# Cross-attention and FFN on one core: the first later group's keys as seven whole block products

## The chip, the cores and the metric

The kernel runs on one NeuronCore of a Trainium2 chip. The core has five engines with instruction queues of their own: TensorE (PE; its weight loads are listed apart as PEld), VectorE (DVE), ScalarE (ACT), GpSimd (POOL) and SyncE (SP, which here only starts transfers). They meet through semaphores. The metric is the device time of one execution in microseconds (us); the median of several executions is compared.

## The reference

The input `x` has 8 sequences of 128 rows by 512. One layer of cross-attention with a context of the same shape, then a gated feed-forward layer, each behind a layer norm, in fp32:

```python
x = x + _L0_xattn_ref(_layernorm(x), ctx_4096, mask, position_bias, ln_weight, w_q, w_k, w_v, w_out)
x = x + _L0_ffn_ref(_layernorm(x), Wg, Wu, Wd, ag, au, ad)
...
h_k = (key_value_states @ w_k.T).reshape(b, lk, H, DH)
h_v = (key_value_states @ w_v.T).reshape(b, lk, H, DH)
score = jnp.einsum('bqhd,bkhd->bhqk', h_q, h_k) + position_bias[None]
score = jax.nn.softmax(jnp.where(m, score, -jnp.inf), axis=-1)
attn = jnp.einsum('bhqk,bkhd->bqhd', score, h_v).reshape(b, lq, H * DH)
out = attn @ w_out.T
```

There are 32 heads of 128, so keys, values and queries are each a product of 1024 by 512 with 512 by 4096. The change touches only how the keys of heads 4 to 7 are computed, not what they are.

## The kernel before

**Groups and stages.** The 32 heads are worked in 8 groups of 4. First come the keys and values of group 0, then the queries of all groups (stored to memory and fetched back in pairs of sequences), then attention, group by group and within a group sequence by sequence (a "batch", b = 0 to 7), then output projection and feed-forward. While group g is in attention, the keys and values of group g+1 are projected in pieces between the batches: in group 0 these are `k1` and `v1`.

**Block products.** A projection is done as a 2 by 2 block product with seven products in place of eight (Winograd's form of Strassen's scheme). The sums of weight blocks, `S`, are made on GpSimd by `combine_rows` (L312); those of the context's blocks were made once. `seven` (L334) runs all seven, in the order 2, 1, 6, 7, 4, 5, 3, each in two tiles of 128 by 512: 14 tiles. A tile goes to a PSUM bank and is read out from there: products 2, 6, 7 and 4 are copied by ACT, products 1, 5 and 3 are added to what is there by VectorE. Product 2 has a pair of banks of its own, products 1, 6, 7 and 4 are accumulated one after the other in a second pair, 5 and 3 in a third. So a tile must wait until the tile before it in its bank has been read out, and only two banks are held at a time.

**Parted products.** `four` (L364) runs only products 1, 6, 7 and 5 as whole tiles: 8 tiles. Products 2, 3 and 4 are parted once more, each into seven small ones, run together by `inner` (L384) in seven steps of three 128x256 products, with two additions on VectorE each. The small products need further sums: of the weights' blocks (`inner_rows` in `later_kv`, L601, eight sums on GpSimd, written to `s_k` or `s_v`) and of the context's blocks (`inner_tokens`, L433, four sums `t_c` on VectorE for each of products 2, 3 and 4, used again by all later groups).

**The order.** `later_kv` (L594) is a generator. Each `next` issues a tile or a step and gives its cost (`FULL` 4 for a tile, `PART` 3 for a step). It also issues what the next pieces need: `begin(n + 1)` makes the `S` of the next projection, and `inner_rows` and `inner_tokens` come at set tiles. For `k1` (n = 0): `begin` of `v1` ahead of tile 4, the context sums of product 4 ahead of tile 5 (those of 2 and 3 ahead of tile 1), `inner_rows` ahead of tile 6. The steps begin behind tile 7 and alternate with tiles; the steps left over run between the tiles of the next projection.

The attention loop (from L889) calls it. In group 0, two tiles are issued ahead of batch 0. In each of batches 0 to 3, `probabilities` (L496) issues the scores `sc` on TensorE, the masked addition `s`, the row maximum `mx` and its negative `nmx` on VectorE, then one piece (`ahead`), the four exponentials on ACT, one piece (`between`), and then `ri`, its reciprocal and `p` on VectorE. `transpose_p` turns `p` in blocks on VectorE (`tt`) and by two transfers through memory (`turned`, `pT`). `advance(3)` multiplies with the values (`av`) three batches later. Further pieces follow until their costs reach `due(g, b)` (L870). For group 0 this is 5, 8, 11 and 14 tiles' cost behind batches 0 to 3; from batch 4 on it runs evenly to the end of the group.

The masks (`s` from `pb` and `mneg`, 128 by 512, on GpSimd) are made two batches ahead into three buffers, so the mask of batch b + 3 waits for `p` of batch b. In batches 0 to 3 of group 0 every engine's instructions are kept in the order of the code (class `InOrder`, L54); most of these rows bear its line, L62.

Of the kernel before, what the change touches and what calls it, by code (L numbers as in the profile page):

```python
# [36 lines left out]
class Later:  # L37
# [10 lines left out]
    def next(self, engine):  # L48
        if self.calls:
            op, args, kw = self.calls.pop(0)  # L50
            getattr(engine, op)(*args, **kw)
# [15 lines left out]
def xattn_ffn_kernel(  # L67
# [26 lines left out]
    NG = H // GH  # L94
# [201 lines left out]
    def sums_a(eng, a11, a12, a21, a22, s1, s2, s4):  # L296

        eng.tensor_tensor(s1, a21, a22, ADD)
        eng.tensor_tensor(s2, s1, a11, SUB)
        eng.tensor_tensor(a21, a11, a21, SUB)  # L300
        eng.tensor_tensor(s4, a12, s2, SUB)
        return {1: a11, 2: a12, 3: s4, 4: a22, 5: s1, 6: s2, 7: a21}
# [9 lines left out]
    def combine_rows(name, w):  # L312

        a11, a12 = w[:, :HC, :HW], w[:, HC:, :HW]
        a21, a22 = w[:, :HC, HW:], w[:, HC:, HW:]
        s = spool.tile([P, 3, HC, HW], F32, tag="S", name=f"S_{name}")
        s1, s2, s4 = s[:, 0], s[:, 1], s[:, 2]
        rows = sums_a(gpsimd, a11, a12, a21, a22, s1, s2, s4)
        rows["lower"] = w[:, HC:]
        return rows  # L320
# [43 lines left out]
    def four(name, product, part, pool=ps_mm, tag="mm"):  # L364

        m = None
        for i, to in ((1, [(1, 1)]), (6, [(1, 2)]), (7, [(2, 2), (2, 1)]), (5, [(2, 2), (1, 2)])):
            if i in (1, 5):
                m = [pool.tile([P, 512], F32, tag=tag, name=f"mm_{name}_{i}_{t}") for t in range(2)]
            for t in range(2):  # L370
                product(i, t, m[t], i in (1, 5))
                for r, c in to:
                    if i == 5:
                        vector.tensor_tensor(part(r, c, t), part(r, c, t), m[t], ADD)
                    else:
                        scalar.copy(part(r, c, t), m[t])  # L376
                yield
# [55 lines left out]
    def inner_tokens(eng, src, half, place, products=SINGLE):  # L433

        blocks = {}
        for n in products:
            b = [src[n][:, c, at] for c in range(2) for at in (slice(0, half), slice(half, None))]
            b11, b12, b21, b22 = b
            t1, t2, t3, t4 = place(n)
            eng.tensor_tensor(t1, b12, b11, SUB)  # L440
            eng.tensor_tensor(t2, b22, t1, SUB)
            eng.tensor_tensor(t3, b22, b12, SUB)
            eng.tensor_tensor(t4, b21, t2, SUB)
            blocks[n] = numbered(*b, t1, t2, t3, t4)
        return blocks
# [143 lines left out]
            yield next(values)  # L589
        yield from values  # L590

    FULL, PART = 4, 3

    def later_kv():  # L594


        def place(n):
            t = ipool.tile([P, 4, HW], F32, tag=f"t{n}", name=f"t_c{n}")
            return (t[:, k] for k in range(4))

        def inner_rows(name, w):  # L601

            s = ipool.tile([P, 3, 3, P], F32, tag="rows", name=f"s_{name}", bufs=2)
            lower = w["lower"].rearrange("p c (n r q) -> p c n r q", n=2, r=2)
            both = [lower[:, c, :, r] for r in range(2) for c in range(2)]
            three = [w[3][:, c, bass.ts(r, P)] for r in range(2) for c in range(2)]
            sums = sums_a(gpsimd, *both, *(s[:, k, :2] for k in range(3)))
            a = {n: {i: rows[:, k] for i, rows in sums.items()} for k, n in enumerate((2, 4))}
            a[3] = sums_a(gpsimd, *three, *(s[:, k, 2] for k in range(3)))
            return a  # L610

        todo = [(g, kind) for g in range(1, NG) for kind in "kv"]
        made, rows = {}, {}

        def begin(n):

            g, kind = todo[n]
            if g not in made:
                made[g] = dict(zip("kv", kv_w.pop(g)))
            rows[n] = combine_rows(f"{kind}{g}", made[g].pop(kind))  # L620

        begin(0)
        b, steps = inner_tokens(vector, ctx_t, HW, place, (2, 3)), iter(())
        for n, (g, kind) in enumerate(todo):
            name, w = f"{kind}{g}", rows.pop(n)
            out = kvs.setdefault(g, ([], []))["kv".index(kind)]
            if g + 1 < NG:
                blocks, smaller = (blocks_T, inner_T) if kind == "k" else (blocks_V, inner_V)
                tiles = four(name, *blocks(name, w, ctx_t, out))
            else:  # L630
                tiles = (project_T if kind == "k" else project_V)(name, w, ctx_t, out)
            for k in itertools.count():

                if k == (3 if n == 0 else 5) and n + 1 < len(todo):
                    begin(n + 1)
                if n == 0 and k == 4:
                    b.update(inner_tokens(vector, ctx_t, HW, place, (4,)))
                if k == (5 if n == 0 else 2) and g + 1 < NG:
                    a = inner_rows(name, w)
                if next(tiles, "none") == "none":  # L640
                    break
                yield FULL
                if k == 6 and g + 1 < NG:
                    steps = smaller(name, a, b, out)
                if next(steps, None):
                    yield PART
# [36 lines left out]
    for n, _ in enumerate(first_kv()):  # L683
        if n in moments_at:
            pair[moments_at[n]] = norm1_moments(moments_at[n])
        if n in scales_at:
            b = scales_at[n]
# [6 lines left out]
        if n in turns_at:  # L694
            b = turns_at[n]
# [174 lines left out]
    def due(g, b):  # L870


        tiles, steps = 2 * 8 * FULL, 2 * 7 * PART
        late = 5 * PART
        if g == 0 and b < 4:
            return (5 + 3 * b) * FULL
        if g < NG - 2:
            start = 14 * FULL if g == 0 else g * (tiles + steps) - late
            end, n, k = (g + 1) * (tiles + steps) - late, 4 if g == 0 else B, b - 4 if g == 0 else b
        else:  # L880
            start, n, k = g * (tiles + steps) - late, B, b
            end = start + late + 25 * FULL
        return start + (end - start) * (k + 1) / n - 1.5

    todo = [(g, i) for g in range(NG) for i in range(B // 2)]
# [3 lines left out]
    for g in range(NG):  # L889
# [6 lines left out]
        if g == 0:  # L896
            products = later_kv()
# [11 lines left out]
        for b in range(B):  # L909
# [49 lines left out]
            if g == NG - 1:  # L959
                while next(products, None):  # L960
                    pass
            else:
                while done < due(g, b):
                    done += next(products)
# [11 lines left out]
            if g == NG - 1:  # L976
# [9 lines left out]
                n = (b + 2) % B, (b + 2) // B  # L986
# [481 lines left out]
```

## Time and profile before

| what | value |
|---|---|
| median of 3 runs | 1083.56 us (1082.39 to 1084.94) |
| the profiled execution | 1083.05 us, of which the span from first to last instruction is 1081.1 us |
| mean granted TensorE clock | 0.998 |
| TensorE in 239.17 to 295.20 us (group 0 in attention) | busy 53.03 of 56.03 us, clock 0.97 |
| TensorE in 295.20 to 355.50 us (group 1) | busy 59.70 of 60.30 us |
| TensorE in 355.50 to 415.70 us (group 2) | busy 60.20 of 60.20 us |

Busy times say how long an engine had an instruction in work. TensorE's rows overlap at their ends, so a group's work is best taken from start to start. A row of the timeline has the start in us, the time in us, the engine, the line, the operation with its result and its sources, and in brackets how long the engine stood idle before it and what released it. A row of the waits has who waited for whom, then the total, the count and the longest.

### The profile page before, as it was taken

Reading aid. Unit: us, or ns where it says so; the run is one execution under the profiler, and the core shown is the slowest. Engines: PE = TensorE matmul, PEld = TensorE weight load, DVE = VectorE, ACT = ScalarE, POOL = GpSimd, SP = SyncE. Lnnn points to the kernel's source line nnn. Section 1 sums busy time; section 2 is a strip of 40 time slices with the busy share of each in tenths; the row PEclk is TensorE's granted clock in tenths of the full one; section 3 lists DMA queues with packets and bytes.
Section 4 is the critical chain, followed back from the end, with each engine's and each line's share of the span. In section 5 each row is a group of like instructions: output and inputs, shape, how many; then the busy total and the mean of one; then the engine's idle time right before and its main releaser. Section 6 shows DMA issues by size and latency. Waiting matters only on the chain.

```text
span 1081.1 us, 14017 instructions
## 1 busy us (share of the span) xinstructions
PE 1070.5 (99%) x4874; PEld 806.3 (75%) x4874; DVE 696.2 (64%) x1280; ACT 331.4 (31%) x902; POOL 463.7 (43%) x519
## 2 busy tenths in 40 slices
PE   9999999998999999999999999999999999999998
PEld 5656666656978788887979768988888865665787
DVE  4653443437888888788877876984444338778732
ACT  2633323213544444444444334221000012332100
POOL 6233454533564545555551363662000326784010
PEclk9999999999999999999999999999999999999999
DMA  9613344453755555465555556873541622110011
GB/s 289 194 58 117 116 159 168 179 190 132 234 203 186 168 171 177 160 205 166 186 186 197 192 177 213 278 242 124 189 142 60 192 103 59 40 49 10 1 39 39
DMA packets 124693, 161.82 MB, mean 150 GB/s; under 512 B 15600, under 2 KB 77296, under 8 KB 124624
## 3 DMA queue, kind: packets, MB, share of 16 engines
q1 hardware_dynamic: 110208, 129.73, 36.4%
q10 hardware_dynamic: 12544, 24.38, 6.3%
q0 software_dynamic: 1872, 6.82, 2.1%
q8 instruction: 39, 0.64, 0.2%
q14 instruction: 30, 0.25, 0.1%
HBM read 104.81 MB, written 56.10 MB: 149 GB/s over the span
## 4 chain that ended last, share of the span: by engine, by line
PE 88%; DVE 6%; DMA 3%; ACT 1%; issue 1%; POOL 0%; SPq 0%; ACTq 0%; DVEq 0%; POOLq 0%
PE mm_q L454 10%; PE m L835 9%; PE mm_v L475 8%; PE mm_k L454 8%; PE m L62 7%; PE d L1389 6%; PE mm_f L1288 6%; PE i_q L403 6%; PE i_v L416 5%; PE i_k L403 4%; PE av L552 4%; PE sc L504 4%; PE i L1254 3%; PE mm_v L62 2%; PE mm_k L62 1%
## 5 line engine op out<-in xcount | busy, mean ns | idle before, releaser
L516 ACT ACTIVATE s<-s,nmx 128x128 f32<-128x128 f32 x240 | 93.3, 390 | 59.4 <-DVE nmx L511 46.8
L493 POOL TENSOR_TENSOR s<-pb,mneg 128x512 f32<-128x512 f32 x40 | 50.9, 1274 | 128.0 <-DVE p L527 104.6
L398 DVE TENSOR_TENSOR q<-q,i_q 128x512 f32<-128x512 f32 x98 | 49.9, 550 | 82.1 <-PE i_q L403 81.7
L557 ACT COPY aT<-av 128x512 f32<-128x512 f32 x60 | 35.1, 586 | 149.9 <-PE av L552 118.1
L527 DVE TENSOR_TENSOR p<-s,ri 128x512 f32<-128x512 f32 x52 | 63.6, 1223 | 1.4
L376 ACT COPY q<-mm_q 128x512 f32<-128x512 f32 x56 | 31.5, 588 | 94.6 <-PE mm_q L454 67.4
L504 PEld LDWEIGHTS sc<-k,q 128*128 128x128 f32 x416 | 54.1, 192 | 8.1 <-issue 6.5
L62 POOL TENSOR_TENSOR s<-pb,mneg 128x512 f32<-128x512 f32 x24 | 30.4, 1272 | 67.3 <-DVE p L527 41.0
L454 PE MATMUL mm_q<-hT,wq 128*128 128x512 f32 x128 | 58.5, 592 | 0.0
L475 PE MATMUL mm_v<-wv,ctx_sb 128*128 128x256 f32 x240 | 56.2, 380 | 0.6 <-ACT v L345 0.6
L454 PE MATMUL mm_q<-hT,S_q 128*128 128x512 f32 x120 | 55.9, 592 | 0.0
L552 PE MATMUL av<-pT,v 128*128 128x128 f32 x416 | 55.1, 275 | 0.6 <-DMA pT<-turned 0.6
L504 PE MATMUL sc<-k,q 128*128 128x128 f32 x416 | 55.3, 275 | 0.0
L62 POOL TENSOR_TENSOR S_q<-wq 128x512 f32<-128x512 f32 x8 | 10.1, 1268 | 104.4 <-ACT wq L62 104.4
L475 PE MATMUL mm_v<-S_v,ctx_sb 128*128 128x256 f32 x232 | 54.6, 380 | 0.0
L398 DVE TENSOR_TENSOR v<-v,i_v 128x512 f32<-128x512 f32 x84 | 43.8, 540 | 13.9 <-PE i_v L416 13.3
L454 PE MATMUL mm_k<-ctx_sb,wk 128*128 128x512 f32 x112 | 52.5, 593 | 0.0
L552 PEld LDWEIGHTS av<-pT,v 128*128 128x128 f32 x416 | 50.6, 192 | 0.8 <-ACT s L516 0.8
L62 PE MATMUL m<-wo,a 128*128 128x256 f32 x200 | 48.8, 380 | 0.9 <-DMA a<-att 0.9
L475 PEld LDWEIGHTS mm_v<-wv,ctx_sb 128*128 128x128 f32 x240 | 44.8, 190 | 6.4 <-ACT v L345 0.8
L454 PE MATMUL mm_k<-ctx_sb,S_k 128*128 128x512 f32 x104 | 48.6, 593 | 0.0
L835 PE MATMUL m<-wo,a 128*128 128x256 f32 x200 | 48.4, 379 | 0.0
(376 smaller groups left out, 2547.1 us busy)
## 6 DMA issues: line engine op xcount, KB each, us to landing
queries<-q SPq DMA_DIRECT2D x32, 512.0 KB, 3.8
turned<-tt SPq DMA_DIRECT2D x64, 256.0 KB, 2.8
pT<-turned SPq DMA_DIRECT2D x64, 256.0 KB, 3.2
att<-aT ACTq DMA_DIRECT2D x64, 256.0 KB, 3.0
q<-queries SPq DMA_DIRECT2D x30, 512.0 KB, 5.1
a<-att SPq DMA_DIRECT2D x23, 512.0 KB, 4.4
wq<-in_wqT_dram SPq DMA_DIRECT2D x8, 1024.0 KB, 6.8
wk<-in_wkT_dram SPq DMA_DIRECT2D x7, 1024.0 KB, 5.4
```

Source lines behind the costliest of these rows:

```text
L62: return self.tc.keep_in_program_order(getattr(self.engine, op)(*args, **kw))
L398: vector.tensor_tensor(to, to, out, ADD)
L403: kv_tensor.matmul(out, a[n][i], b[n][i], start=first, stop=True, skip_group_check=True)
L454: kv_tensor.matmul(out, w[i][:, c, bass.ts(t, P)], src[i][:, c, :], start=(first and c == 0), stop=(c == HC - 1), skip_group_check=True,)
L475: kv_tensor.matmul(out[:, bass.ts(k, HW)], src[i][:, c, bass.ts(2 * t + k, S)], w[i][:, c, :], start=(first and k == 0 and c == 0), stop=( ...
L504: tensor.matmul(sc[:, j, :], qT[:, j, bass.ts(b % 2, S)], kT[j][:, cols], start=True, stop=True)
L516: scalar.activation(s[:, j, :], s[:, j, :], AF.Exp, bias=nmx[:, j : j + 1], accum_out=sm[:, j : j + 1],)
L527: vector.tensor_tensor(p.rearrange("q h (j r) -> q h j r", r=BS), s.rearrange("q h (r j) -> q h j r", r=BS), ri.unsqueeze(2).unsqueeze(3). ...
L552: tensor.matmul(av[:, j, :], v[b // 2][:, b % 2, bass.ts(j, P)], pT[:, :, j, :], start=True, stop=True,)
L835: tensor.matmul(m[n], sa[n][:, c, :], wo_t[g][n][:, c, :], start=(g == order[0] and c == 0 and PRODUCTS.index(n) % 2 == 0), stop=(g == ord ...
L1288: nc.tensor.matmul(out, ws[t][n][:, c, :], h2_t[n][:, :, c, :], start=(first and c == 0), stop=(c == HC - 1), skip_group_check=True,)
L1389: nc.tensor.matmul(out, lhs, rhs, start=bank not in started, stop=(i == NP - 1 or n == 8), skip_group_check=True,)
```

## The change

`k1`, the first projection that `later_kv` makes (n = 0), now runs through `seven` in 14 whole tiles rather than through `four` and seven steps of small products. All others stay parted (but those of the last group, which were whole before). `begin` of `v1` stands ahead of tile 6 rather than tile 4. The context sums of product 4 stand ahead of tile 11 rather than tile 5. `inner_rows` isn't called for `k1`. A tile of `k1` is counted at 3.8 (`FIRST`), and the due costs of the first four batches are counted in it too.

```diff
--- before.py
+++ after.py
@@ -589,7 +589,9 @@
             yield next(values)
         yield from values
 
-    FULL, PART = 4, 3
+
+
+    FULL, PART, FIRST = 4, 3, 3.8
 
     def later_kv():
 
@@ -624,23 +626,24 @@
         for n, (g, kind) in enumerate(todo):
             name, w = f"{kind}{g}", rows.pop(n)
             out = kvs.setdefault(g, ([], []))["kv".index(kind)]
-            if g + 1 < NG:
+            parted = 0 < n and g + 1 < NG
+            if parted:
                 blocks, smaller = (blocks_T, inner_T) if kind == "k" else (blocks_V, inner_V)
                 tiles = four(name, *blocks(name, w, ctx_t, out))
             else:
                 tiles = (project_T if kind == "k" else project_V)(name, w, ctx_t, out)
             for k in itertools.count():
 
-                if k == (3 if n == 0 else 5) and n + 1 < len(todo):
+                if k == 5 and n + 1 < len(todo):
                     begin(n + 1)
-                if n == 0 and k == 4:
+                if n == 0 and k == 10:
                     b.update(inner_tokens(vector, ctx_t, HW, place, (4,)))
-                if k == (5 if n == 0 else 2) and g + 1 < NG:
+                if k == 2 and parted:
                     a = inner_rows(name, w)
                 if next(tiles, "none") == "none":
                     break
-                yield FULL
-                if k == 6 and g + 1 < NG:
+                yield FULL if n else FIRST
+                if k == 6 and parted:
                     steps = smaller(name, a, b, out)
                 if next(steps, None):
                     yield PART
@@ -873,7 +876,7 @@
         tiles, steps = 2 * 8 * FULL, 2 * 7 * PART
         late = 5 * PART
         if g == 0 and b < 4:
-            return (5 + 3 * b) * FULL
+            return (5 + 3 * b) * FIRST
         if g < NG - 2:
             start = 14 * FULL if g == 0 else g * (tiles + steps) - late
             end, n, k = (g + 1) * (tiles + steps) - late, 4 if g == 0 else B, b - 4 if g == 0 else b
```

## The prediction

> **What bounds the kernel now.** I read the page's busy shares first, then TensorE's own list of waits, then the timeline around those waits.
>
> ```profile
> PE 1070.5 (99%) x4874; PEld 806.3 (75%) x4874; DVE 696.2 (64%) x1280; ACT 331.4 (31%) x902; POOL 463.7 (43%) x519
> ...
> PE i_k L62 <- DVE k L62: 2.0, 1, 2.0
> PE i_k L403 <- POOL s L62: 1.0, 1, 1.0
> PE av L552 <- DMA pT<-turned: 0.6, 1, 0.6
> ```
>
> TensorE is busy 99% of the span, so work added to it costs its own length, and a stall removed is gained in full. Of the few stalls, the three shown lie in the stretch that the change rewrites: at 264.48, 260.93 and 296.87 us. The table of stretches (length, then busy times, then granted clock, DMA share, GB/s) shows a second loss:
>
> ```profile
> 257.90:265.00 7.10, 4.10 (x18) 3.01 (x17) 6.61 (x13) 1.11 (x6) 1.27 (x1) 1.00 0.24 76
> 265.00:270.00 5.00, 5.00 (x21) 4.45 (x20) 4.25 (x8) 1.05 (x5) 2.68 (x4) 0.66 0.14 52
> ```
>
> In half-microsecond stretches the clock is 0.50 from 265.5 to 268.9. From start to start the loss is: 1.14 us (259.79 to 260.93), 2.26 us (262.22 to 264.48), and at half clock 5.67 us for 3.90 us of work, 1.77. Together **5.2 us**, and 0.6 at 296.87. From 239.01 to the first scores of the next group at 295.0 there are 56.0 us; 50.8 of them are work.
>
> Why it stalls: the small products' additions stand in VectorE's strict order behind one batch's softmax and the four context sums `t_c`, and VectorE is busy 6.61 of 7.10 us.
>
> ```profile
> 250.48 1.27 POOL L62 TENSOR_TENSOR s<-pb,mneg 128x512 f32<-128x512 f32 x1 [11.28 <-DVE p L62]
> 251.00 1.03 DVE L62 TENSOR_TENSOR t_c<-ctx_sb 128x256 f32<-128x256 f32 x1
> 251.71 0.91 POOL L62 TENSOR_TENSOR s_k<-wk 128x256 f32<-128x256 f32 x1
> 252.06 0.83 DVE L62 TENSOR_TENSOR t_c<-ctx_sb,t_c 128x256 f32<-128x256 f32 x1
> ...
> 254.55 0.68 DVE L62 TENSOR_TENSOR s<-sc,s 128x512 f32<-128x512 f32 x1
> ...
> 278.54 1.28 POOL L62 TENSOR_TENSOR wk<-wk 128x512 f32<-128x512 f32 x1
> ...
> 278.97 0.87 DVE L523 TENSOR_SCALAR ri<-sm 128x4 f32<-128x4 f32 x1 [0.80 <-ACT s L516]
> ...
> 279.76 1.28 POOL L62 TENSOR_TENSOR S_k<-wk,S_k 128x512 f32<-128x512 f32 x1
> ...
> 280.08 1.83 DVE L527 TENSOR_TENSOR p<-s,ri 128x512 f32<-128x512 f32 x1
> ```
>
> Each of these VectorE rows ends after the GpSimd row that was running when it began. Beside an idle GpSimd `t_c` took 0.42 (239.71), `ri` 0.17 and `p` 1.09 (249.24). Four `t_c` took 3.55 us here; at the 0.35 spacing seen at 239.71 they would take 1.5.
>
> **TensorE's work.** A whole tile is 4 rows in 1.72 us, a small step 6 rows in 1.29. Before: 8 tiles and 7 steps, 13.76 + 9.03 = 22.8. After: 14 tiles, 24.1. **Plus 1.3 us**, and nothing hides it. Here a rule pulls the other way: the Trainium skill, "TensorE: Matmul & The Clock Gate", section "Back-to-back issue gap", gives sustained spacings of 131 ns at 512 columns and 81 at 128 (98 at 256, my linear estimate), so long matmuls are cheaper per column. By it the 24 long rows that replace 42 short ones would take 0.77 of their time, 6.9 us for 9.0, a gain of 2.1. In the rows here 512 columns take 0.43 us and 256 take 0.215: no discount. I take the row.
>
> **What is removed elsewhere.** 14 additions on VectorE and 8 small sums on GpSimd leave; VectorE's whole-tile additions rise from 4 to 6, ACT keeps 8 copies. These engines are not the bound on average; what counts is the order in which their pieces stand. No DMA is issued by the moved sums. The key weights are last read by tile 10 (about 259) and not by a step at 276.7, so the load behind them (SP at 277.39) can start earlier; its first reader is at 328, so that is worth nothing.
>
> **What is moved.** (a) The keys' smaller row sums go, and the value rows' four sums `S_v` (234.12 to 239.2 before, 1.27 each) move behind tile 5. On GpSimd they now follow the fourth mask, which waits for the first `p`. (b) The last four `t_c` move from behind the first batch to behind the third, ahead of tile 11's addition. (c) The order of products is now 2, 1, 6, 7, 4, 5, 3: product 3 is accumulated in product 5's bank, so **tile 13 waits for tile 11's addition** on VectorE.
>
> Now the order, in the durations of the rows. TensorE: tiles 1 and 2 until 242.44, scores 0 until 243.33, tiles 3, 4, 5 until 248.5, scores 1 (0.885) and tiles 6 to 8 until 254.5, scores 2 and tiles 9 to 11 until 260.6, scores 3 and tile 12 until 263.2. The copies on ACT come in time for all of these (the table load at 245.85 starts as soon as ACT is free, so it moves ahead of the first exponentials).
>
> VectorE: tile 4's addition ends at 247.7, `ri`, reciprocal, `p` (1.09) and transpose end at 250.0, against 251.08 before. Batch 1 takes 5.6 us (254.55 to 260.2 before) when nothing collides. But the fourth mask now runs 249.4 to 250.7 and `S_v` 250.7 to 255.85: `nmx` waits about 0.4, `ri` 0.6 and `p` 0.9, less what the pieces hide: end at 257.5 and not at 255.9, **1.6 us of collision**. Batch 2: 5.6, until 263.1. Its mask runs from 262.5, and right behind it on GpSimd follow the values' smaller row sums, which wait for nothing (they did so at 268.47, behind the mask of 267.24). So `t_c` stands beside the same pair as at 250.48: 3.55 us rather than 2.0 beside the mask alone, **1.5 us of collision**, until 266.65; tile 11's addition ends at 267.3. Tile 13 was ready at 263.2: **stall 4.1 us**. Bounds: 1.0 with neither collision, 4.6 if `p` waits a whole GpSimd row. I take 4.1, since both collisions are in the rows.
>
> The clock: the gap of 2.0 us brought 3.4 us at 0.50, the one of 0.98 nothing. The same page, section "Why this matters for your kernels", puts the limit at gaps of about 3 us; by that the old gap cost no clock, and the row contradicts it. The new gap is beyond both: 3.4 us at half clock, **1.7 us** (1.2 to 3.4, by where the gap meets the clock's own stretches).
>
> Behind it: tile 14 and scores 4 follow with VectorE ahead of them. Value tile 3 waits for ACT's copy of tile 1, which stands behind the exponentials of batch 4; `nmx` of that batch meets GpSimd's next sums at about 275. With half clock behind TensorE this is covered: 0.2 (0 to 1.7 if the clock stays whole). The wait at 296.87 goes: batch 5's `p` is about 2 us earlier relative to its use; kept, it costs 0.6.
>
> **The sum.** +1.3 work, +4.1 stall, +1.7 clock, +0.2 copy, -5.2 old stalls and clock, -0.6: **+1.5 us**. The groups behind show no idle TensorE between 300 and 580, so it is carried to the end. On the profiled execution's 1083.05 this gives **1084.6**. The median of the runs shown is 0.5 above that execution, inside their spread; I don't add it.
>
> **Rivals.**
> 1. *The collisions fail to happen* (the row sums stand elsewhere on GpSimd than I read). The stall is 1.0, the clock stays whole, the copy costs 0.6: 1.3 + 1.0 + 0.6 - 5.8 = -2.9, 1080.1. For it: 8 of VectorE's additions in net leave exactly this stretch. Against: the order on GpSimd is kept as written, and the rows show the waiting.
> 2. *Only the first collision.* Stall 2.6, clock whole as the page has it, copy 0.4: -1.5, 1081.5. By the row of 265.5 the clock halves and it is about 1083.2. The value sums' start at 268.47 speaks against.
> 3. *Slower: the gap at tile 13 spans a boundary of the clock's stretches*, so the clock is still judged idle once more and stays at half for 6.8 us: 1.3 + 4.1 + 3.4 + 0.2 - 5.8 = +3.2, 1086.3. It decides from 5.2 us at half clock on (cost 2.6). For it: a gap longer than 3.4 us must leave idle time in two stretches. Against: after the old gap one stretch was enough.
> 4. *That the change doesn't take the stalls away at all* is excluded in the place (the small steps of the keys are gone), not in the amount: that is the forecast.
>
> **Chances.** The forecast has 0.42, its own range 1083.2 to 1086.1; rival 3 has 0.22, rival 1 0.20, rival 2 0.16. A difference under 0.2% (2.2 us) of the median can't be told from none with this kernel. Faster: rival 1 and a quarter of rival 2, 0.24. Within: 0.24 of the forecast and the rest of rival 2, 0.36. Slower: 0.18 of the forecast and rival 3, 0.40. The range, 1080.3 to 1087.0, leaves out about half of rival 1 and a third of rival 3.
>
> **What would show it.** No small key products in the first group, 24.1 us of whole key tiles; one wait of 3.5 to 4.5 us at tile 13, its releaser an addition on VectorE; `t_c` at 0.8 to 1.0 each beside GpSimd; `p` of batch 1 at about 1.9; the clock at 0.50 for some 3.4 us behind 267; no wait of `av` at the head of the next group; that group's first scores at 296 to 297. If the wait at tile 13 is under 2 us, or the clock stays at 1.00, the forecast is wrong and the kernel is faster.

## The result, and the profile after

| | before | after |
|---|---|---|
| median (22 executions each) | 1083.32 us (1082.02 to 1085.54) | 1086.12 us (1084.01 to 1091.25) |
| the profiled execution, its span | 1083.05, 1081.1 us | 1087.1, 1085.3 us |
| tile 1 of the second group's keys starts at | 239.01 us | 239.19 us |
| the third group's second key tile (group 1's piece) starts at | 300.89 us | 305.54 us |

The ratio of the times is 1.0026 (1.0019 to 1.0034): the change costs 2.8 us, of which the prediction had 1.5. From the first key tile to the second key tile behind the head of group 1 the two profiled executions took 61.88 and 66.35 us. These 4.5 us are the whole difference of the profiles: further on no place adds to it (at 919 us it is 4.2).

First the page's busy shares of the kernel after, in the columns of before:

```profile
PE 1072.6 (99%) x4856; PEld 803.6 (74%) x4856; DVE 693.7 (64%) x1268; ACT 331.4 (31%) x902; POOL 458.7 (42%) x511
```

TensorE still shows 99%. The share cannot show the loss: an instruction at half clock counts as busy for about twice as long (a key tile took 3.25 us at 301.12 and 1.88 at 305.54). TensorE's waits between 239 and 306 us (total, count, longest) do show one part of it:

```profile
PE mm_k L62 <- DVE k L62: 3.6, 1, 3.6
PE av L552 <- DMA pT<-turned: 1.9, 1, 1.9
```

The three waits of before have become two, and both are longer. The table of stretches (length; busy PE, PEld, DVE, ACT, POOL; clock; DMA share; GB/s) shows what each brought with it:

```profile
257.90:265.00 7.10, 7.10 (x24) 3.48 (x22) 5.12 (x10) 2.70 (x10) 2.22 (x2) 1.00 0.44 142
265.00:270.00 5.00, 1.38 (x4) 0.50 (x4) 4.93 (x7) 0.00 (x0) 4.84 (x8) 0.97 0.62 226
270.00:274.00 4.00, 4.00 (x13) 2.63 (x12) 3.11 (x7) 2.17 (x9) 0.54 (x2) 0.61 0.01 2
300.00:302.50 2.50, 2.50 (x10) 1.79 (x10) 2.50 (x5) 0.58 (x1) 2.42 (x5) 0.59 0.35 105
302.50:305.00 2.50, 2.50 (x11) 1.42 (x10) 1.00 (x3) 0.60 (x2) 2.50 (x4) 0.73 0.54 196
```

The stretch to 265 us, where before was idle for 3 of 7.1 us, is now full. The loss sits behind it: TensorE works 1.38 of 5 us, and VectorE and GpSimd are busy beside each other in nearly all of it. Then the clock is halved, twice: from 269.73 to 273.14 and from 300.45 to 303.86 us. The timeline gives the causes (start, time, engine, line, operation; in brackets the idle time before and its releaser):

```profile
243.51 1.95 PE L416 MATMUL i_v<-wv,ctx_sb 128*128 128x128 f32 x16
...
256.25 1.27 POOL L62 TENSOR_TENSOR S_v<-wv,S_v 128x512 f32<-128x512 f32 x1
256.57 1.81 DVE L62 TENSOR_TENSOR p<-s,ri 128x512 f32<-128x512 f32 x1
...
264.05 1.26 POOL L62 TENSOR_TENSOR s<-pb,mneg 128x512 f32<-128x512 f32 x1 [4.25 <-DVE p L62]
264.57 1.02 DVE L62 TENSOR_TENSOR t_c<-ctx_sb 128x256 f32<-128x256 f32 x1
265.27 0.90 POOL L62 TENSOR_TENSOR s_v<-wv 128x256 f32<-128x256 f32 x1
265.63 0.83 DVE L62 TENSOR_TENSOR t_c<-ctx_sb,t_c 128x256 f32<-128x256 f32 x1
...
268.11 0.68 DVE L62 TENSOR_TENSOR k<-k,mm_k 128x512 f32<-128x512 f32 x1
...
268.93 2.97 PE L62 MATMUL mm_k<-ctx_sb,S_k 128*128 128x512 f32 x4 [3.62 <-DVE k L62]
...
289.25 0.71 DVE L270 STREAM_TRANSPOSE tt<-p 128x512 f32<-128x512 f32 x1
289.30 1.44 SPq L870 DMA_DIRECT2D q<-queries  x1
290.85 0.59 SPq L272 DMA_DIRECT2D turned<-tt  x1
...
296.45 0.36 SPq L277 DMA_DIRECT2D pT<-turned  x1
299.83 1.49 PE L552 MATMUL av<-pT,v 128*128 128x128 f32 x8 [1.90 <-DMA pT<-turned]
```

The reader is to see two chains. In the middle: `p` of batch 1 takes 1.81 us beside the last `S_v`; two batches later the four `t_c` run from 264.57 to 268.1 beside the mask and the value rows' `s_v`, tile 11's addition follows them, and tile 13 starts 0.8 us behind the start of that addition. At the ends: 16 rows of small value products (`i_v`), which the code issues only behind batch 7, were carried out at 243.51, ahead of tile 3, and 50 us later `av` of batch 5 waits 1.90 us for its transfer. That second chain was not foreseen. In the kernel before it reads:

```profile
287.84 0.70 DVE L270 STREAM_TRANSPOSE tt<-p 128x512 f32<-128x512 f32 x1
288.61 0.59 SPq L272 DMA_DIRECT2D turned<-tt  x1
...
296.87 1.13 PE L552 MATMUL av<-pT,v 128*128 128x128 f32 x8 [0.60 <-DMA pT<-turned]
```

From the end of the transpose to `av` it took 8.3 us before and 9.9 after. TensorE was free for `av` 7.7 us behind the transpose before and 8.0 after. So against before the wait grew because the transfers took longer, and not because TensorE came sooner; 0.8 us of the 1.5 are that `turned` left 0.07 us behind its transpose before and 0.89 after.

The spread of after is wide. Its executions fall apart by their mean granted clock: 12 at 0.998 with a median of 1085.1 us, 4 at 0.997 with 1086.6, 6 at 0.995 with 1088.7. One stretch of 3.4 us at half clock takes 0.0016 from the mean of 1085 us, so these means fit about one, two and three stretches; only the profiled execution (0.997) has a trace that shows where its two are.

### The profile page after: what moved, and what is told of

It is laid out like the page before. It is cut to its first block, busy times and chain, and to the rows that moved or that the text cites. A ratio compares the mean times of both kernels' runs of the same rounds, so it can differ in the third digit from the quotient of the medians.

```text
span 1085.3 us, 13958 instructions
## 1 busy us (share of the span) xinstructions
PE 1072.6 (99%) x4856; PEld 803.6 (74%) x4856; DVE 693.7 (64%) x1268; ACT 331.4 (31%) x902; POOL 458.7 (42%) x511
## 4 chain that ended last, share of the span: by engine, by line
PE 89%; DVE 5%; DMA 3%; ACT 1%; issue 1%; POOL 0%; SPq 0%; ACTq 0%; DVEq 0%; POOLq 0%
PE mm_q L454 10%; PE m L838 9%; PE mm_v L475 8%; PE mm_k L454 8%; PE m L62 7%; PE d L1392 6%; PE mm_f L1291 6%; PE i_q L403 6%; PE i_v L416 5%; PE i_k L403 4%; PE av L552 4%; PE sc L504 4%; PE i L1257 3%; PE mm_k L62 2%; PE mm_v L62 2%; PE mm_q L62 1%
## 5 line engine op out<-in xcount | busy, mean ns | idle before, releaser
L398 DVE TENSOR_TENSOR v<-v,i_v 128x512 f32<-128x512 f32 (+1 forms) x84 | 44.0, 542 | 15.8 <-PE i_v L416 15.1
```

Of the source, the lines that this page charges most:

```text
L398: vector.tensor_tensor(to, to, out, ADD)
```

## The experiments

For each of the kernels one execution was profiled. Because the later part of a span has its own chances, the table splits it: A from tile 1 to the second key tile behind the head of group 1, B from there to the start of the output projection's `m` that waits for `att` (758.89 us in before), and in B the waits of `m` for the last output weights, `wo`. Each ratio is to executions of before taken beside that kernel.

| kernel | median, us | ratio to before | A, us | B, us | waits for `wo`, us |
|---|---|---|---|---|---|
| before | 1083.32 | 1 | 61.88 | 458.00 | 0 |
| after | 1086.12 | 1.0026 | 66.35 | 457.51 | 0 |
| sums_behind_keys | 1082.21 | 0.9984 (0.9976 to 0.9992) | 59.48 | 460.54 | 1.38 |
| value_sums_early | 1086.19 | 1.0028 (1.0016 to 1.004) | 66.62 | 458.89 | 0.58 |
| values_not_ahead | 1086.15 | 1.0023 (1.0014 to 1.0033) | 64.14 | 460.09 | 1.05 |
| row_sums_late | 1087.24 | 1.0037 (1.0023 to 1.0051) | 65.55 | 460.37 | 1.01 |
| sums_first | 1079.83 | 0.9959 (0.9947 to 0.9972) | 58.34 | 459.65 | 0.57 |
| sums_behind_values_held | 1081.89 | 0.998 (0.9974 to 0.9987) | 59.11 | 461.22 | 1.10 |
| sums_behind_all_held | 1079.81 | 0.9961 (0.9949 to 0.9974) | 57.88 | 458.70 | 0 |
| parted_sums_first | 1079.45 | 0.9958 (0.9945 to 0.9972) | 57.69 | 458.18 | 0 |
| whole_without_waits | 1078.5 | 0.9954 (0.994 to 0.9968) | 56.98 | 458.23 | 0 |
| parted_sums_first_2 | 1080.11 | 0.9964 (0.9951 to 0.9977) | 58.47 | 458.91 | 0.54 |

B is 457.5 to 458.7 us where no `wo` is waited for and 458.9 to 461.2 where it is, and the waits don't go with A: the same kernel, run twice as parted_sums_first, shows them once. They go with a longer B, but the waits themselves (0.5 to 1.4 us) are only a part of what it is longer by; what makes up the rest is not shown. So B is not laid to the change here.

Diffs are against the kernel after unless said otherwise.

**sums_behind_keys.** The last context sums leave the queue ahead of tile 11's addition and stand behind the keys, where the parted values first need them.

```diff
-                if n == 0 and k == 10:
-                    b.update(inner_tokens(vector, ctx_t, HW, place, (4,)))
+                if n == 1 and k == 2:
+                    b.update(inner_tokens(InOrder(tc, nc.vector), ctx_t, HW, place, (4,)))
```

> The four last context sums stand behind the keys' last tile (in batch 4) and no longer ahead of tile 11's addition. Theory (the stall at tile 13 is VectorE's queue, with the context sums in it): the wait at tile 13 falls from 3.6 us to under 0.6, the half clock behind it goes, and the time falls by 3 to 5 us. Rival (the loss is mostly the 1.3 us of longer matmul work and the wait for pT at the head of the next group): the wait at tile 13 may go, but the time falls by less than 1 us, since later waits take it up.

Measured: 1082.21 us, 3.9 below after and 1.2 below before. TensorE's waits between 239 and 306 us:

```profile
PE av L552 <- DMA pT<-turned: 1.1, 2, 0.9
PE mm_v L475 <- ACT v L376: 0.3, 1, 0.3
```

And the stretch in which after lost its time:

```profile
262.00:280.00 18.00, 17.94 (x94) 13.68 (x94) 13.90 (x24) 7.15 (x25) 14.02 (x15) 1.00 0.58 192
```

The wait at tile 13 is gone and so is the half clock: TensorE works 17.94 of 18 us at 1.00. The position of four small instructions on VectorE is what the change lost by, not the whole tiles.

**value_sums_early.** `S_v` goes back to its place ahead of tile 4, so that batch 1's softmax does not meet it.

```diff
-                if k == 5 and n + 1 < len(todo):
+                if k == (3 if n == 0 else 5) and n + 1 < len(todo):
                     begin(n + 1)
```

> The value rows' sums S_v are begun ahead of tile 4 again, as in the kernel before; all else as changed. Theory (collisions with GpSimd lengthen batch 1 on VectorE): p of batch 1 at 1.1 us and not 1.8, ri at 0.2 and not 0.8, nmx at 0.2 and not 0.6; the wait at tile 13 falls by about 1.6 us, to 2.0; half clock behind it stays; time down by about 1.5. Rival (GpSimd's place is without effect): wait at tile 13 as before, 3.6 us, same time.

Measured: 1086.19 us, the same as after. `p` of batch 1 takes 1.08 us and `ri` 0.17, so the collision was real and is gone. But the waits became these:

```profile
PE av L552 <- DMA pT<-turned: 2.8, 1, 2.8
PE mm_k L62 <- DVE k L62: 2.6, 1, 2.6
PE mm_v L475 <- ACT v L376: 0.2, 1, 0.2
```

With `S_v` made earlier, 24 rows of small value products instead of 16 ran ahead of tile 3, and `av` of batch 5 waits 2.75 us instead of 1.90. A is even 0.3 longer. What was taken from one wait came back in the other, and both still halve the clock. The expected time was missed. The median hides two kinds of execution: three of the twelve show a clock of 1.0 and a median of 1084.4 us, eight 0.997, as the profile, and 1087.4.

**values_not_ahead.** The pieces of the values keep the order of the code to the end of the group, so none can run ahead of the keys.

```diff
             if (g, b) == (0, 3):
                 tensor, vector, scalar = nc.tensor, nc.vector, nc.scalar
+            if (g, b) == (0, B - 1):
                 kv_tensor = tensor
```

> The small value products (16 rows of i_v, 1.8 us) that now run ahead of tile 3 are held at their place in batch 7. Theory (pulled ahead, they shorten the stretch between batch 5's p and its use, so the wait for pT at the head of the next group grows to 1.9 us): that wait falls to under 0.6 us and the half clock behind it goes, while the wait at tile 13 grows to 4 to 5 us, because the tiles come earlier and the softmax doesn't by as much; time down by 2 to 3 us. Rival (that wait is the transfers' own, slowed by other loads): it stays at 1.5 to 2 us and the time stays.

Measured: 1086.15 us; the expected gain did not show in the median. Two lines of TensorE's waits, over the whole span:

```profile
PE mm_k L62 <- DVE k L62: 4.0, 1, 4.0
...
PE m L62 <- POOL wo L62: 1.1, 1, 1.1
```

The stretches around tile 13, for TensorE alone, cut where the clock changes and 3.4 us apart (length; busy; clock; DMA share; GB/s):

```profile
262.61:266.03 3.42, 1.33 (x4) 1.00 1.03 363
266.03:269.44 3.41, 1.46 (x2) 0.50 0.34 105
269.44:272.85 3.41, 3.41 (x10) 0.50 0.00 0
```

The wait of `av` has gone altogether, and with it the half clock behind it. Two things moved, though: TensorE comes to `av` 9.5 us behind the transpose (8.0 in after), and `turned` leaves 0.03 us behind it (0.89 in after). This run does not part them; sums_behind_values_held, below, does. At the place where it was expected the gain is there, A is 2.2 us shorter. It would be 3.6 by the two losses that went, but the stall at tile 13 is 0.4 longer, a copy is waited for 0.2, and the clock is at half for 6.8 us (266.03 to 272.85) instead of 3.4; TensorE worked in 4.9 of these, which costs 2.4 us instead of 1.7. Behind A the rest was lost, 2.6 us more in B than after, with 1.05 of it an open wait for `wo`. This is one profiled execution; that the other executions lost it in the same place is not shown.

**row_sums_late.** The value rows' small sums `s_v` move behind tile 5 of the values, so that `t_c` meets only the mask.

```diff
-                if k == 2 and parted:
+                if k == (5 if n == 1 else 2) and parted:
                     a = inner_rows(name, w)
```

> The values' smaller row sums s_v stand behind the mask of batch 6 on GpSimd, no longer beside the context sums. Theory (second collision): the four context sums take about 2.0 us from first to last and not 3.6, the wait at tile 13 falls by about 1.5 us to 2.1, with half clock behind it; time down by about 1.5 us. Rival: context sums as long as before, same wait, same time.

Measured: 1087.24 us. The four `t_c` took 1.02, 0.42, 0.42 and 0.42, as expected. The waits:

```profile
PE av L552 <- DMA pT<-turned: 4.3, 2, 3.1
PE mm_k L62 <- DVE k L62: 2.2, 1, 2.2
```

And the mask on GpSimd, the queue of the transfers and its wait, where TensorE's new waits come from:

```profile
283.94 1.27 POOL L62 TENSOR_TENSOR s<-pb,mneg 128x512 f32<-128x512 f32 x1
285.24 0.37 SPq L865 DMA_DIRECT2D pb<-in_pbias_dram  x1
285.65 0.50 SPq L272 DMA_DIRECT2D turned<-tt  x1
...
SPq L865 <- POOL s L62: 9.7, 1, 9.7
```

The stall at tile 13 fell from 3.6 to 2.2 and brought no half clock. But the sums now stand on GpSimd from 278.57 to 283.99, beside batch 4's `p` (1.40 us; 1.11 in after) and ahead of a mask. That mask follows them at 283.94. On SP a load of the biases waits for it, and behind that load stands batch 4's transposed `p`: ready at 281.7, it was sent at 285.65 only. `av` then waited 3.11 us at 293.54, with a half clock behind it, and 1.14 at 300.76. The collision was real, but what the sums delay in their new place was not foreseen, and the time grew.

**sums_first.** All twelve context sums are made ahead of batch 0, where GpSimd is idle.

```diff
-        b, steps = inner_tokens(vector, ctx_t, HW, place, (2, 3)), iter(())
+        b, steps = inner_tokens(vector, ctx_t, HW, place), iter(())
...
-                if n == 0 and k == 10:
-                    b.update(inner_tokens(vector, ctx_t, HW, place, (4,)))
```

> As changed, but all twelve context sums stand ahead of batch 0, where GpSimd is idle. Theory (the four sums cost what VectorE's queue and GpSimd make of them at their place): they take 1.4 us there, which batch 0 hides behind tile 4's addition, so the wait at tile 13 falls from 3.6 to under 0.6 us as with the sums behind the keys, and batch 4 isn't lengthened either: 1081.0 to 1082.3 us. Rival (each microsecond on VectorE in the first batches counts, wherever it stands): wait at tile 13 of 1.5 us or more, with half clock, 1083 us or more.

Measured: 1079.83 us, better than expected. The `t_c` take 0.42 us each, tile 13 doesn't wait, the clock is whole; one wait of `av`, 0.81 us at 293.42, is left.

**sums_behind_values_held** (sums_behind_keys with values_not_ahead) and **sums_behind_all_held** (both with value_sums_early).

> The four sums behind the keys' last tile, and the small value products held in batch 7. Theory (the two waits are separate: one is VectorE's queue, the other the room between p and its use): no wait for pT at the head of the next group, wait at tile 13 at 0.3 to 1.0 us, clock whole; 1081 to 1082 us. Rival (what leaves one wait comes back at the other, because the chain of softmaxes sets the pace of the stretch): wait at tile 13 over 1.5 us, and no faster than the sums behind the keys alone (1082.2).

> The four sums behind the keys' last tile, the small value products held in batch 7, and S_v begun ahead of tile 4. Theory: the chain of softmaxes is 1.6 us shorter without the collision in batch 1, so no wait over 0.3 us is left in the group; 1080.3 to 1081.3 us, which is the cost of whole tiles alone above a kernel without stalls. Rival (the collision in batch 1 is hidden by now): same as without it, within 0.4 us.

Measured: 1081.89 and 1079.81 us. The first is no faster than sums_behind_keys beyond the spread: in its place stand waits of 0.48 and 0.25 us at the keys and 0.66 of `av` of batch 4, and its profiled execution waited 1.10 us for `wo`. It does part the two causes left open above: here as in sums_behind_keys `turned` of batch 5 leaves 0.03 us behind its transpose, TensorE comes to `av` 8.2 us behind it rather than 6.8, and the wait of 0.89 us there is gone. So holding the value products takes that wait away by itself. The second has a single wait of note, 0.66 us of `av`. So `S_v` placed early, worth nothing by itself, is worth 1.2 us of A once the other two causes are gone.

**parted_sums_first.** The same step from the kernel before, with the parted keys: is the gain the whole tiles' or the sums'?

```diff
-        b, steps = inner_tokens(vector, ctx_t, HW, place, (2, 3)), iter(())
+        b, steps = inner_tokens(vector, ctx_t, HW, place), iter(())
...
-                if n == 0 and k == 4:
-                    b.update(inner_tokens(vector, ctx_t, HW, place, (4,)))
```

> The kernel before, with its parted key products, and only the four context sums moved ahead of batch 0. Theory (the old stalls too were VectorE's queue with the context sums in it, and whole tiles only add 1.3 us of matmul): the waits of 1.0 and 2.0 us at the small key products and the half clock fall to under 1 us in sum; 1078.5 to 1080.5 us, faster than every kernel with whole tiles. Rival (the small products' own additions made the stall, so it needs whole tiles): waits of 2 us or more stay, 1082 us or more.

Measured: 1079.45 us, as fast as the whole tiles with the sums first. Most of the gain over before comes from the place of the sums alone.

**whole_without_waits** (sums_first, value_sums_early and values_not_ahead together) beside **parted_sums_first_2** (parted_sums_first again, on the same chip).

> As changed, with all context sums first, S_v ahead of tile 4 and the small value products held in batch 7: every cause found for a wait is taken out, whole key tiles stay. Theory (what is left of the change is its matmul work, 1.3 us): 0.8 to 1.5 us slower than the parted kernel with its sums first, run beside it. Rival (VectorE's relief by 12 additions pays for the work): within 0.4 us of it or faster.

> The kernel before with its context sums first, a second time, beside the whole tiles without waits. By the first run: 1079.5 us, 0.4% under the kernel before. By the theory the faster of the two by 0.8 to 1.5 us; by the rival no faster than the other.

Measured: 1078.5 us (1077.53 to 1081.06) and 1080.11 us (1078.71 to 1081.96). The same stretch of the first:

```profile
239.20:300.00 60.80, 60.80 (x303) 43.74 (x303) 46.12 (x92) 28.81 (x97) 28.01 (x32) 1.00 0.60 207
```

and of the second:

```profile
239.20:300.00 60.80, 59.02 (x310) 45.57 (x309) 51.10 (x102) 28.66 (x97) 32.07 (x39) 1.00 0.61 204
```

With whole tiles TensorE is never idle in 60.8 us; with parted ones it stands still for 1.78 us, 1.31 of it in one wait of `av` for `pT`, and in the first profile of the same kernel for 1.01. VectorE is busy for 5.0 us less with whole tiles. By these profiles the surplus of matrix work is paid back by waits that do not arise; that it is VectorE's relief which removes them is argued, not shown. The intervals of the two overlap, so which is faster isn't settled; that whole tiles are slower by their surplus, as the theory had it, does not show. whole_without_waits is the fastest kernel measured, 0.46% below before and 0.7% below after.

## Why the prediction was right or wrong

- **The work, +1.3 us.** Of the right size. whole_without_waits does the same tiles with no wait in 56.98 us of A; before's A without its 5.8 us of loss is 56.1. By that the work is +0.9, by the rows +1.3; the rule that long matmuls are cheaper, which would have made it -2.1 in place of +1.3, isn't borne out here. (The first scores of the next group, read at 295.0 in the prediction, are at 295.21: 51.0 of 56.2 us are work. The sum does not use that.)
- **The collisions and the stall at tile 13, +4.1.** Right: `p` of batch 1 1.81 us (1.9 predicted), the four `t_c` 3.6 us (3.55), tile 13 ready at 265.16 and started at 268.93, 3.8 us. value_sums_early and row_sums_late removed one collision each, and the stall fell to 2.6 and 2.2; sums_behind_keys removed the `t_c` and with them the stall. All this stood some 1.8 us later than predicted, by the small value products at 243.51, which moved TensorE and VectorE alike and so left the stall's size.
- **Half clock, +1.7.** Right at tile 13, 3.4 us at 0.50, but that it was one such stretch was luck: it hangs on where the gap falls (last section). Rival 3, two of these stretches at one gap, is not what after's profile shows there; values_not_ahead shows it, at 2.4 us and not the 3.4 of the rival's sum, as TensorE stood idle in a part of them.
- **The copy, +0.2.** Not seen: value tile 3 waited for nothing.
- **"The wait at 296.87 goes", -0.6. This step failed.** The wait became 1.90 us, +1.3, and brought 1.7 us of half clock, which the sum did not have at all. Up to the first scores of group 1, after is 1.5 us behind before (57.69 us from tile 1, for 56.20), where the other terms give 2.1. From there to the second key tile it loses 3.0 more, and these two are all of it. The prediction counted with `p` of batch 5 about 2 us earlier relative to its use. It was 0.2 earlier (8.0 us for 7.7), since 1.8 us of the work that lay between them had moved ahead of tile 3. And the transfers, for which the sum had no term, took 1.5 us longer: `turned` was issued at 290.85, 0.9 us after its transpose was done, behind a load of queries on SP; why the other 0.7 us were longer is not shown. With that work held in its place the wait is gone (values_not_ahead, and without the delay on SP sums_behind_values_held). Why the order laid down at build time pulled value products forward here, and none in before, is not shown; that whole tiles leave free the PSUM banks of `i_k` is a guess that no run tested.
- **The table load on ACT "moves ahead of the first exponentials".** Wrong: at 245.75 it stood idle for 2.30 us until `nmx` was there, and the first exponentials ended at 248.7. Tile 4's addition was late for another reason, so it cost nothing.
- **The size.** Executions of after at a mean clock of 0.998 have a median of 1085.1 us, 1.8 above before's median, near the +1.5. That nearness is in part luck, for the work and the stall came out smaller and the wait of `av` larger than in the sum. What lies above is the clock, to judge by the granted clock alone: the steps between the medians of the three sets of executions, 1.5 and 2.1 us, are near the 1.7 of a stretch. Before has such a mix too: of the 70 executions beside the experiments 32 show 0.998, as its profile, and 36 show 1.0, so the 1.8 us of half clock that the sum takes off were there in about half of them only.

## What to carry to other kernels

Sums that are needed later don't belong in a strict queue ahead of an addition that the bottleneck waits for: make them where their engine and its neighbour are idle. Where a softmax chain sets the pace, a wait that is removed alone can come back at another place (value_sums_early, and by way of the transfers' queue row_sums_late; sums_behind_keys kept its gain), so look for all of its causes and take them away together. Before a slower but simpler form of a computation is judged, count what it spares the second engine: here about 1 us of surplus work on TensorE (0.9 by the runs, 1.3 by the rows) stood beside 5 us less on VectorE, and no loss of time showed.

## What the hardware showed that was not expected

Whether a gap halves the clock depends on where it falls, not on its length alone. In the twelve traces every time between two changes of the granted clock is a whole number of 3.413 us (76, 1 and 238 of them in before, 77, 1, 8, 1 and 229 in after), so the clock changes only at points that lie 3.41 us apart. Cut at such points, after and then row_sums_late read (TensorE alone; length; busy; clock; DMA share; GB/s):

```profile
262.90:266.31 3.41, 2.41 (x11) 1.00 1.01 344
266.31:269.73 3.42, 0.80 (x2) 1.00 0.45 157
269.73:273.14 3.41, 3.41 (x10) 0.50 0.08 23
...
262.42:265.83 3.41, 2.94 (x13) 1.00 0.87 285
265.83:269.24 3.41, 1.72 (x4) 1.00 0.46 176
269.24:272.66 3.42, 3.42 (x17) 1.00 0.45 149
```

In after the gap of 3.62 us ahead of tile 13 leaves TensorE idle for 1.00 us of one stretch and 2.62 of the next, and one stretch at half clock follows. In row_sums_late the gap of 2.16 us is split into 0.47 and 1.69, and none follows. In values_not_ahead the gap of 4.04 us is split into 2.09 and 1.95, and two follow, the first while TensorE still stands idle. Over the twelve profiles, from 10 to 1070 us, eight stretches have 1.90 us of idle time or more, and each is followed by one at 0.50; in all others it is 1.69 or less, and none is. So the limit here lies between 1.69 and 1.90 us of idle time in one stretch of 3.41 us. The limit of about 3 us, which the prediction weighed against the row of before, doesn't hold here.

A stall of some 2 us thus costs up to 1.7 us more behind it or nothing, by where it falls. The clocks of before's executions, 0.998 in some and 1.0 in others, fit that. So a change that leaves a gap of this size is judged from many executions and their granted clocks, not from one profile.
